# A graph layer on one core: two groups of edges move from GpSimd's gather to hand copies, and the first loads are issued earlier

## The chip, the core and the metric

The kernel runs on one core of a Trainium2 chip. The core has TensorE (PE in the profile; PEld is its weight load), VectorE (DVE), ScalarE (ACT), GpSimd (POOL) and SyncE (SP), each with an instruction stream of its own that runs strictly in order, and 16 DMA engines that move data between HBM and the core's own memory. The metric is device time of one execution in microseconds (us). Three runs of the kernel before took 3376.49, 3378.95 and 3381.35 us; the median, 3378.95 us, is the time before.

## What is computed

One message-passing layer over N = 12,500 nodes and E = 400,000 edges, sorted by target node `dst`. Cut to what matters:

```python
h = relu(layernorm(x))                                  # N x 128
m = relu(concat(h[src], h[dst], edge_attr) @ w1 + b1) @ w2 + b2
agg = segment_sum(m, dst)                               # N x 128
# a GRU cell with input agg and state h, and a residual
gi, gh = agg @ w_ih + b_ih, h @ w_hh + b_hh
r, z = sigmoid(gi_r + gh_r), sigmoid(gi_z + gh_z)
n = tanh(gi_n + r * gh_n)
out = x + (1 - z) * n + z * h
```

`src` is random, so `h[src]` is a gather of 400,000 rows. `dst` is sorted, so the edges of a stretch have their targets in a small window of nodes.

## The kernel before, in words

**First stage (lines 354 to 488).** A loop over chunks `q` of four blocks of 128 nodes normalizes x, keeps hᵀ for all nodes in `hT_all` (128 features on the partitions, one column of 4 bytes for each node), and stores A = h·w1a and B = h·w1b + b1 in HBM. A row of A is what the source of an edge adds to its hidden layer, a row of B what its target adds. `batch_store` (line 253) writes the first three batches of B in this stage; later batches come from the node steps. `at_row` (line 419) loads the source numbers of the groups that are fetched by hand, three rows for each q.

**Edges.** The edges are cut in NP = 391 groups of 1024 (`PAIR` = 8 tiles of 128; group 0 has 5 tiles), and each group is two units u = 2k, 2k+1, so there are NU = 782 units. The main loop (line 1075) goes over u; `stages(u)` (line 1040) holds the work of several units at different depths: the one-hot of target places (`onehot_T`, `onehot`), the products of `pre(u + 3)`, the sums of `add(u + 2)` or `relu(u + 2)`; `seg(u)` then sums over the edges of a node. Everything is in program order on each engine; nothing is reordered at run time. Seven steps `u = -7 .. -1` of `stages` fill the pipe.

For each group three loads are needed. `fetch(q)` (line 567) brings the target places and edge features of two groups to a tile `L`, two DMAs on SP's queue. `window_rows(k)` (line 600) brings the 32-row windows of B to `RW[k % 4]`, two DMAs on SP's queue, from addresses that SP reads to registers, a block of 14 groups at a time. The third is the source part, by one of four ways (`mode`, line 91):

- *GpSimd's gather* (the groups not in `mode`): `gather(k)` (line 151) issues 8 indirect DMAs on POOL, one for each tile of 128 edges, to one of GBUFS = 11 buffers `G`. The first RAW = 9 groups gather rows of x, which are normalized on the spot, since A is not there yet; all others gather rows of A. VectorE adds them in `add` (line 713), behind a wait for their landing.
- *ScalarE by hand* ("act", 28 groups): ACT copies one column of `hT_all` for each of the 1024 edges, at an address in a register (line 979), to `HE_act`; PE then multiplies it by w1a (line 694) and ACT applies the relu (line 725) in place of VectorE's addition.
- *VectorE by hand* ("dve", 27 groups): as ACT, but two columns of bytes in an instruction (line 986), and a copy that puts the bytes in order for each 128 edges (line 991), to `HE_dve`.
- *SP by hand* ("sp", 5 groups): 1024 single-row DMAs from A (line 968) to `G_sp`; VectorE adds as for GpSimd.

A hand job for group k is spread evenly over the units from the end of the engine's job before (`START` for the first: unit 4 for ACT, 14 for DVE) to unit 2k - 4 (`run_jobs`, line 1007: four times in each unit, so many steps that the job is done on time). Before, the groups of ACT end with 374 and 388, those of DVE with 372 and 386, those of SP with 306 and 379. Each hand tile has two buffers, except `G_sp`.

**Nodes.** The targets are cut in 29 blocks (14 groups each but for the last two). When a block's groups are done, `node(b)` (line 790) is run in small steps, one or two units apart: sums over the windows, the gates on PE, sigmoid and tanh on ACT, products on DVE, and the next batch of B. `last_node` (line 857) does the last block.

**Order at the end of the first stage (lines 1032 to 1037):** the first gathers of A, `dst_tile(1)`, three fetches, four `window_rows`; then the seven filling steps.

Of the kernel before, what the change touches and what calls it, by code (L numbers as in the profile page):

```python
# [52 lines left out]
PIECE = 128  # L53
STEP = {"act": 4, "dve": 8, "sp": 4}
ROW = 4 * D
SPREAD = {"dve": 27, "act": 28, "sp": 5}
START = {"dve": 14, "act": 4, "sp": 24}
NR = 12672

H_AT = 16512  # L60

# [2 lines left out]
def tile_gnn(ctx: ExitStack, tc: tile.TileContext, x, src, srcT, dstT, dstP, eaT, eaP, w1, b1, w2T, b2,  # L64
# [23 lines left out]
        return [(t0 + a * GRP + j, j, a) for j in (2 * h, 2 * h + 1) for a in range(2)  # L88
                if t0 + a * GRP + j < t1]

    mode, order = {}, {m: [] for m in SPREAD}
    for m, n in SPREAD.items():
        lo, hi = START[m] // 2 + 2, NP - {"dve": 5, "act": 3, "sp": 12}[m]
        for i in range(n):
            k = lo + int((i + 1) * (hi - lo) / n)
            while k in mode:
                k += 1
            mode[k] = m
            order[m].append(k)


    src_i = {}
# [86 lines left out]
    nc.vector.memset(brow, 0.0)  # L189
    b1b = const.tile([128, D], F32, name="b1b")  # L190
    base_d = at[96:97, :NP - 1]
    by_hand = [k for m in ("sp", "act", "dve") for k in order[m]]
    NJ = len(by_hand)
    place_of = const.tile([NJ, 2], F32, name="place_of")
    for i, (to_sp, to_others) in enumerate(((ROW, 4), (0, H_AT))):
# [107 lines left out]
    def setup(pool):  # L303
# [45 lines left out]
        yield  # L349
        place(0)  # L350

    st_all = const.tile([128, NT, 2], F32, name="st_all")
    nc.vector.memset(st_all[:, NFULL, :], 0.0)
    with tc.tile_pool(name="pp", bufs=3) as pp:
# [85 lines left out]
        for q in range(NC + 3):  # L440
            if q < NC:
                b, i0, c, e, P, n0 = chunk(q)
                if c == 0:
                    stat(b + 2)
                    fin(b + 1)
            if 1 <= q <= NC:
                b, i0, c, e, P, n0 = chunk(q - 1)
                pts[q - 1] = SEGB[q % 2]
                for j in range(c, e):
                    nc.tensor.transpose(pts[q - 1][:, (j - c) * P:(j - c + 1) * P],  # L450
                                        xs[b][:P, j, :], ident[:P, :P])
                if e == bats[b][1]:
                    load(b + 5)
            if q >= 3:
                b, i0, c, e, P, n0 = chunk(q - 3)
                if c == 0:
                    asb[b] = pp.tile([128, 8, D], F32, name="asb", bufs=2)
                nc.scalar.copy(asb[b][:P, c:e, :], pas.pop(q - 3)[:P, :e - c, :])
            if q < NC:
                b, i0, c, e, P, n0 = chunk(q)  # L460
                for j in range(c, e):
                    relu_norm(xs[b][:P, j, :], xs[b][:P, j, :], st_all[:P, i0 + j, :])
                if e == bats[b][1]:
                    sqr(b + 2)
            if 1 <= q <= NC:
                b, i0, c, e, P, n0 = chunk(q - 1)
                copy = nc.scalar.copy if q % 4 == 0 else nc.vector.tensor_copy
                copy(columns(b, c, e), pts.pop(q - 1)[:, :(e - c) * P].rearrange(
                    "f (i p) -> f i p", i=e - c))
            if q >= 4:  # L470
                for _ in range(3):
                    at_row()
            if q >= 6:
                next(setting, None)
            if q in (6, 8, 10):
                batch_product(q // 2 - 3, pp, "bt", 1)
            if q in (7, 9, 11):
                batch_store(q // 2 - 3)
            if q >= 3:
                b, i0, c, e, P, n0 = chunk(q - 3)  # L480
                if e == bats[b][1]:
                    nc.sync.dma_start(nodes(A, i0, e, P), asb[b][:P, :e, :])
            if 2 <= q <= NC + 1:
                b, i0, c, e, P, n0 = chunk(q - 2)
                pas[q - 2] = ps2.tile([128, PAIR, D], F32, name="pre")
                for j in range(c, e):
                    nc.tensor.matmul(pas[q - 2][:P, j - c, :], columns(b, j, j + 1)[:, 0, :],
                                     w1a, start=True, stop=True)
# [72 lines left out]
        nc.vector.tensor_copy(flag, f[:, 6:7])  # L561


    Ls, OH, RT, HE, SEG = ({} for _ in range(5))
    hand = {}

    def fetch(q):
        if q * QP >= NP:
            return
        n = min(QP, NP - q * QP)  # L570
        c = slice(q * QP * 512, (q * QP + n) * 512)
        Ls[q] = p3.tile([128, QP * 512], F32, name="L")
        p = dstP[:, c]
        nc.sync.dma_start(
            Ls[q].bitcast(I32)[:2 * V, :n * 512],
            bass.AP(tensor=p.tensor, offset=p.offset, ap=[list(p.ap[0]), [0, V], [1, n * 512]]))
        nc.sync.dma_start(Ls[q][2 * V:, :n * 512], eaP[:, c])

    def onehot_T(k):
        if k >= NP:  # L580
# [8 lines left out]
                                    accum_out=dlast[:2 * V, n:n + 1])  # L589


    bases = {}

    def block(k):
        return max(b for b in range(NB) if BLOCKS[b][0] <= k)

    def slot(b, i):
        return i // 2 if b < NB - 1 else (BP - BLOCKS[b][1]) // 2 + i // 2

    def window_rows(k):  # L600
        if k >= NP:
            return
        b = block(k)
        k0, n, _ = BLOCKS[b]
        if k == k0:
            _, vals = nc.values_load_multi_w_load_instructions(
                base_i[0:1, b, 0:n], engines=[ET.SP], min_val=0, max_val=4 * D * LAST,
                skip_runtime_bounds_check_because="clamped above")
            for i, v in enumerate(vals):
                bases[k + i] = v  # L610
        v = bases.pop(k)
        for a in range(2):
            nc.sync.dma_start(RW[k % 4].bitcast(U8)[V * a:V * (a + 1), a, :],
                              B_bytes[bass.ds(v + 4 * D * SHIFT * a, 4 * D * V)].rearrange(
                                  "(p f) -> p f", p=V))

    def onehot(k):
        if k >= NP or (k % 2 and k > 1):
# [330 lines left out]
    def one_by_one(m, k):  # L949
        et = {"act": ET.Activation, "dve": ET.DVE, "sp": ET.SP}[m]  # L950
        r = by_hand.index(k)
        if m == "sp":
            goal[k] = tc.alloc_semaphore(f"brought{r}"), 16 * PAIR * 128
            G[k] = pj.tile([128, GRP, 2, D], F32, name="G_sp", bufs=1)
            rows = G[k].bitcast(U8)
        else:
            hand[k] = pj.tile([128, PAIR * 128], F32, name=f"HE_{m}")
            he = hand[k].bitcast(U8)
        for e0 in range(0, PAIR * 128, LOAD[m]):
            low, high = (0, ROW * (N - 1)) if m == "sp" else (H_AT, H_AT + 4 * (N - 1))  # L960
            _, vals = nc.values_load_multi_w_load_instructions(
                at[r:r + 1, e0:e0 + LOAD[m]], engines=[et], min_val=low, max_val=high,
                skip_runtime_bounds_check_because="src holds numbers of nodes")
            if m == "sp":
                for i, v in enumerate(vals):
                    e = e0 + i
                    a, j = divmod(e // 128, GRP)
                    fetched = nc.sync.dma_start(rows[e % 128:e % 128 + 1, j, a, :],
                                                A_bytes[bass.ds(v, ROW)].rearrange("(o f) -> o f", o=1))
                    fetched.then_inc(goal[k][0], 16)  # L970
                    tc.no_tile_sem_insts.add(fetched.ins.name)
                    tc.add_to_no_dep_group(f"rows{k}", fetched.ins)
                    if i % STEP[m] == STEP[m] - 1:
                        yield
                continue
            if m == "act":
                for i, v in enumerate(vals):
                    e = e0 + i
                    nc.scalar.copy(he[:, e * 4:e * 4 + 4], column(v))  # L979
                    if i % STEP[m] == STEP[m] - 1:  # L980
                        yield
                continue
            if e0 % PIECE == 0:
                both = pj.tile([128, PIECE // 2, 4], U16, name="both")
            for i in range(0, LOAD[m], 2):
                nc.vector.scalar_tensor_tensor(both[:, (e0 % PIECE + i) // 2, :], column(vals[i + 1]),  # L986
                                               256.0, column(vals[i]), op0=ALU.mult, op1=ALU.add)
                if i % STEP[m] == STEP[m] - 2:
                    if (e0 + i + 2) % PIECE == 0:
                        p0 = e0 + LOAD[m] - PIECE  # L990
                        nc.vector.tensor_copy(  # L991
                            he[:, p0 * 4:(p0 + PIECE) * 4].rearrange("p (n c b) -> p n c b", c=2, b=4),
                            both.bitcast(U8).rearrange("p n (b c) -> p n c b", c=2))
                    yield
# [12 lines left out]
    def run_jobs(u, phase):  # L1007
        if phase == 0:
            for m, k, span in jobs.get(u, ()):
                live[m] = [one_by_one(m, k), u, span, PAIR * 128 // STEP[m], 0]  # L1010
        for m, job in list(live.items()):
            it, start, span, steps, done = job
            want = -(-steps * ((u - start) * PH + phase + 1) // (span * PH))
# [16 lines left out]
            pass  # L1030

    gathers(0)
    dst_tile(1)
    for q in range(3):
        fetch(q)
    for k in range(4):
        window_rows(k)


    def stages(u):  # L1040
# [248 lines left out]
```

## Time and profile before

| | us |
|---|---|
| median of the runs | 3378.95 |
| the profiled execution, its own time | 3383.87 |
| its span (first to last instruction) | 3382.1 |
| granted TensorE clock, mean over the span | 0.795 of full |
| ACT busy | 3081.1 |
| POOL busy | 2542.8 |
| PE busy (matmuls) | 2400.4 |
| DVE busy | 2213.6 |

The page of the profile has the busy time of each engine, its groups of instructions by line with the mean time of one, and what ended the engine's idle time before them. "issue" there means that the engine waited for no other work that the profile shows, but for its own instruction stream (reading registers, making up a DMA). The timeline has instructions in order of time, neighbours of one kind merged; the number in square brackets is the idle time before, with the instruction that ended it. A table of windows has the busy time of each engine in a stretch of the span.

### The profile page before, as it was taken

The numbers are of one execution on the slowest core, as the hardware profiler recorded it, in microseconds if no ns is written. First come the engines' busy times: TensorE is split into PE (matmuls) and PEld (weight loads), VectorE is DVE, ScalarE is ACT, GpSimd is POOL, SyncE is SP. The second block draws the span as 40 slices with busy tenths as digits, with TensorE's granted clock in tenths as the row PEclk, the third lists the DMA queues.
The fourth block names the chain that finished last, engine by engine and source line by source line (L and its number), as shares of the span: only waits on it lengthen the run. The fifth ranks groups of instructions, "written<-read, shape, count | busy, mean of one in ns | idle before, by whom it ended". The sixth has DMA issues, their size and how long they took to land. (4 is left out here: it accounts for less than half of the span.)

```text
span 3382.1 us, 93395 instructions
## 1 busy us (share of the span) xinstructions
PE 2400.4 (71%) x13113; PEld 1554.8 (46%) x13113; DVE 2213.6 (65%) x16274; ACT 3081.1 (91%) x29057; POOL 2542.8 (75%) x2654
## 2 busy tenths in 40 slices
PE   7567766776677677668776777677667767766767
PEld 6444444444444444445444444444444444444445
DVE  8566666766666666666667766666656666666665
ACT  7599899999999998998999999999889998988975
POOL 7777777777777777777777777777777777777775
PEclk9778777887888777877877878787777787778778
DMA  6433444444444444444444444444444444343332
GB/s 215 104 92 84 95 99 101 99 97 103 96 95 99 97 98 95 99 104 97 96 98 97 98 95 105 97 99 98 95 98 96 100 95 99 94 96 94 92 94 67
DMA packets 196737, 335.77 MB, mean 99 GB/s; under 512 B 69445, under 2 KB 118148, under 8 KB 196112
## 3 DMA queue, kind: packets, MB, share of 16 engines
q0 software_dynamic: 84640, 173.51, 23.0%
q1 hardware_dynamic: 111327, 156.18, 17.8%
q14 instruction: 517, 4.23, 0.4%
q8 instruction: 109, 1.79, 0.2%
q10 hardware_dynamic: 144, 0.07, 0.0%
HBM read 309.25 MB, written 20.24 MB: 97 GB/s over the span
## 5 line engine op out<-in xcount | busy, mean ns | idle before, releaser
L163 POOL DMA_INDIRECT G<-A,src_i x2576 | 2475.8, 961 | 790.4 <-issue 761.2
L979 ACT COPY HE_act<-hT_all 128x4 uint8 x28672 | 2889.0, 189 | 52.9 <-issue 29.1
L986 DVE SCALAR_TENSOR_TENSOR both<-hT_all 128x4 uint16 x13824 | 1174.3, 154 | 930.3 <-issue 925.6
L683 PE MATMUL pre<-RW,L 128*128 128x256 f32 x3128 | 1136.1, 489 | 461.3 <-DMA RW<-B 237.7
L683 PEld LDWEIGHTS pre<-RW,L 128*128 128x128 f32 x3128 | 662.8, 237 | 736.8 <-issue 420.2
L739 PE MATMUL seg<-RB,OH 128*32 128x129 f32 x6250 | 592.7, 319 | 244.2 <-DVE RB L713 211.9
L739 PEld LDWEIGHTS seg<-RB,OH 128*32 128x32 f32 x6250 | 328.0, 123 | 590.7 <-DVE RB L713 310.1
L713 DVE CUSTOM_DVE_ANT_0 RB<-pre,G 128x1024 f32<-128x1024 f32 x323 | 391.1, 1211 | 70.9 <-DMA G<-A,src_i 56.5
L586 DVE TENSOR_SCALAR L<-L,node_of 64x512 f32<-64x512 int32 x382 | 185.9, 487 | 62.2 <-DMA L<-in_dstP 59.9
L725 ACT ACTIVATE RB<-pre 128x1024 f32<-128x1024 f32 x64 | 65.0, 1016 | 91.0 <-PE pre L694 91.0
L633 DVE TENSOR_TENSOR OH<-dloc,seg 128x512 f32<-128x512 f16 (+1 forms) x198 | 132.3, 669 | 0.0
L765 PE MATMUL nd<-spot,sums 128*128 128x40 f32 x782 | 119.6, 326 | 3.6 <-DVE sums L748 3.6
L765 PEld LDWEIGHTS nd<-spot,sums 128*128 128x128 f32 x782 | 115.5, 237 | 12.7 <-issue 8.8
L991 DVE COPY HE_dve<-both 128x512 uint8<-128x512 uint8 x216 | 97.6, 452 | 7.4
L244 PE MATMUL nd<-w1b,hT_all 128*128 128x128 f32 x224 | 49.4, 368 | 73.1 <-DVE xb L850 73.1
L734 PE MATMUL seg<-zrow 1*128 1x129 bf16 x196 | 45.5, 232 | 78.1 <-DVE OH L633 78.0
L694 PEld LDWEIGHTS pre<-w1a,HE_dve 128*128 128x128 f32 x432 | 89.1, 255 | 12.4
L694 PEld LDWEIGHTS pre<-w1a,HE_act 128*128 128x128 f32 x448 | 85.9, 238 | 11.0
L694 PE MATMUL pre<-w1a,HE_dve 128*128 128x128 f32 x432 | 85.4, 333 | 0.0
L694 PE MATMUL pre<-w1a,HE_act 128*128 128x128 f32 x448 | 83.7, 319 | 0.0
L163 POOL DMA_INDIRECT G<-in_x,src_i x69 | 65.6, 950 | 21.9 <-issue 20.7
L244 PEld LDWEIGHTS nd<-w1b,hT_all 128*128 128x128 f32 x224 | 35.2, 231 | 85.5 <-DVE xb L850 80.0
(177 smaller groups left out, 1346.2 us busy)
## 6 DMA issues: line engine op xcount, KB each, us to landing
G_sp<-A SPq DMA_DIRECT2D x5120, 0.5 KB
L<-in_dstP SPq DMA_DIRECT2D x195, 256.0 KB
L<-in_eaP SPq DMA_DIRECT2D x195, 256.0 KB
G<-A,src_i POOLq DMA_INDIRECT x2576, 2.5
RW<-B SPq DMA_DIRECT2D x782, 16.0 KB
xb<-in_x SPq DMA_DIRECT2D x26, 256.0 KB
out<-xb SPq DMA_DIRECT2D x26, 256.0 KB
xs<-in_x SPq DMA_DIRECT2D x11, 512.0 KB
```

The lines of the kernel that those rows point to most:

```text
L163: fetched = nc.gpsimd.indirect_dma_start(out=G[k][:, j, a, :], out_offset=None, in_=table, in_offset=bass.IndirectOffsetOnAxis(ap=src_i[c] ...
L244: nc.tensor.matmul(pm[:m, i:i + D], hT_all[:, n0 + i:n0 + i + m], w1b, start=True, stop=True)
L586: nc.vector.tensor_scalar(o, i, node_of[:, k:k + 1], None, op0=ALU.is_equal)
L633: nc.vector.tensor_tensor(p, dloc[:, e0:e1, None].to_broadcast(shape), row[:, None, :].to_broadcast(shape), op=ALU.is_equal)
L683: nc.tensor.matmul(p[:, 2 * i:2 * i + 2, :], Ls[k // QP][:, c0:c0 + 128], RW[k % 4], start=True, stop=not raw)
L694: nc.tensor.matmul(p[:, 2 * i + a, :], cols, w1a, start=False, stop=n + 1 == len(l) or l[n + 1][1] != j)
L713: made = nc.vector._custom_dve(TENSOR_ADD_SAT, out=o, in0=p, in1=G[k].rearrange("p j a f -> p (j a) f")[:, c, :], s0=float("inf"), s1=0.0)
L739: nc.tensor.matmul(p[r0:r0 + V, :D + 1], OH[k][:, a * GRP + j, :], RB[k % 2][:, 2 * j + a, :D + 1], start=False, stop=all(b != a for _, _, ...
L765: nc.tensor.matmul(p[:, bass.ds(offs[i], V + SHIFT)], sums[:, slot(b, i), :D], spot[:, i % 2, :], start=False, stop=i == len(offs) - 1)
L979: nc.scalar.copy(he[:, e * 4:e * 4 + 4], column(v))
L986: nc.vector.scalar_tensor_tensor(both[:, (e0 % PIECE + i) // 2, :], column(vals[i + 1]), 256.0, column(vals[i]), op0=ALU.mult, op1=ALU.add)
L991: nc.vector.tensor_copy(he[:, p0 * 4:(p0 + PIECE) * 4].rearrange("p (n c b) -> p n c b", c=2, b=4), both.bitcast(U8).rearrange("p n (b c) ...
```

## The change

Two things are changed.

1. *The first loads.* `fetch(0)` is issued at q = 4 of the first stage, on ScalarE's queue, to a buffer of `HE_dve` (the tile pool of `L` does not exist yet at that point). The four first `window_rows` are issued at q = 16 of that stage, on SP's queue as before. After the first stage only `fetch(1)` and `fetch(2)` are left, now ahead of `dst_tile(1)`.
2. *The groups by hand.* ACT gets 29 groups in place of 28, DVE 27 as before, and both share group 385 (`SHARED` = NP - 6): ACT copies its edges 0 to 511 and DVE its edges 512 to 1023, to one tile `HE_dve`. GpSimd's gather thus has two groups fewer. The jobs are spread anew so that both engines end with group 385: ACT's jobs are 13 groups apart in most cases (13 or 14 before, 13.7 on the average), DVE's 13 or 14 (14 before). ACT's last jobs are 365, 379 and half of 385; DVE's 364, 378 and half of 385; SP's five are 85, 156, 228, 299, 371. Groups 386 to 390 all go to GpSimd.

```diff
-SPREAD = {"dve": 27, "act": 28, "sp": 5}
+SPREAD = {"dve": 27, "act": 29, "sp": 5}
 START = {"dve": 14, "act": 4, "sp": 24}
+SHARED, CUT = NP - 6, 512
...
-    mode, order = {}, {m: [] for m in SPREAD}
+    def share(m, k):
+        return (0, PAIR * 128) if k != SHARED else (0, CUT) if m == "act" else (CUT, PAIR * 128)
+
+    mode, order = {SHARED: "both"}, {m: [] for m in SPREAD}
     for m, n in SPREAD.items():
-        lo, hi = START[m] // 2 + 2, NP - {"dve": 5, "act": 3, "sp": 12}[m]
+        lo, hi = START[m] // 2 + 2, NP - 20
+        part = 0
+        if m != "sp":
+            hi, part = SHARED, (share(m, SHARED)[1] - share(m, SHARED)[0]) / (PAIR * 128)
         for i in range(n):
-            k = lo + int((i + 1) * (hi - lo) / n)
+            k = lo + int((i + 1) * (hi - lo) / (n + part))
             while k in mode:
                 k += 1
             mode[k] = m
             order[m].append(k)
+        order[m] += [SHARED] if part else []
...
+        if q == 0:
+            Ls[q] = pj.tile([128, QP * 512], F32, name="HE_dve")
+        else:
+            Ls[q] = p3.tile([128, QP * 512], F32, name="L")
         p = dstP[:, c]
+        queue = nc.scalar if q == 0 else nc.sync
...
+            if q == 16:
+                for k in range(4):
+                    window_rows(k)
+            if q == 4:
+                fetch(0)
...
-            hand[k] = pj.tile([128, PAIR * 128], F32, name=f"HE_{m}")
+            if k not in hand:
+                hand[k] = pj.tile([128, PAIR * 128], F32, name="HE_dve" if k == SHARED else f"HE_{m}")
...
-        for e0 in range(0, PAIR * 128, LOAD[m]):
+        for e0 in range(*share(m, k), LOAD[m]):
...
     gathers(0)
+    for q in (1, 2):
+        fetch(q)
     dst_tile(1)
-    for q in range(3):
-        fetch(q)
-    for k in range(4):
-        window_rows(k)
```

The definitions of `fetch`, `window_rows`, `block` and `bases` move ahead of the first stage, otherwise unchanged.

More of the change, by code (lines that the diff above doesn't have):

```diff
@@ L191, in tile_gnn @@
     base_d = at[96:97, :NP - 1]
-    by_hand = [k for m in ("sp", "act", "dve") for k in order[m]]
+    by_hand = order["sp"] + order["act"] + [k for k in order["dve"] if k != SHARED]
     NJ = len(by_hand)
@@ L350, in setup, with fetch, block, window_rows @@
         place(0)
+    Ls = {}
+    def fetch(q):
+        if q * QP >= NP:
+            return
+        n = min(QP, NP - q * QP)
+        c = slice(q * QP * 512, (q * QP + n) * 512)
+        if q == 0:
+            Ls[q] = pj.tile([128, QP * 512], F32, name="HE_dve")
+        else:
+            Ls[q] = p3.tile([128, QP * 512], F32, name="L")
+        p = dstP[:, c]
+        queue = nc.scalar if q == 0 else nc.sync
+        queue.dma_start(
+            Ls[q].bitcast(I32)[:2 * V, :n * 512],
+            bass.AP(tensor=p.tensor, offset=p.offset, ap=[list(p.ap[0]), [0, V], [1, n * 512]]))
+        queue.dma_start(Ls[q][2 * V:, :n * 512], eaP[:, c])
+    bases = {}
+    def block(k):
+        return max(b for b in range(NB) if BLOCKS[b][0] <= k)
+    def window_rows(k):
+        if k >= NP:
+            return
+        b = block(k)
+        k0, n, _ = BLOCKS[b]
+        if k == k0:
+            _, vals = nc.values_load_multi_w_load_instructions(
+                base_i[0:1, b, 0:n], engines=[ET.SP], min_val=0, max_val=4 * D * LAST,
+                skip_runtime_bounds_check_because="clamped above")
+            for i, v in enumerate(vals):
+                bases[k + i] = v
+        v = bases.pop(k)
+        for a in range(2):
+            nc.sync.dma_start(RW[k % 4].bitcast(U8)[V * a:V * (a + 1), a, :],
+                              B_bytes[bass.ds(v + 4 * D * SHIFT * a, 4 * D * V)].rearrange(
+                                  "(p f) -> p f", p=V))
     st_all = const.tile([128, NT, 2], F32, name="st_all")
@@ L561, in check_windows @@
         nc.vector.tensor_copy(flag, f[:, 6:7])
-    Ls, OH, RT, HE, SEG = ({} for _ in range(5))
+    OH, RT, HE, SEG = ({} for _ in range(4))
     hand = {}
[L567 to L577, printed above, removed]
     def onehot_T(k):
@@ L589, in onehot_T @@
                                     accum_out=dlast[:2 * V, n:n + 1])
-    bases = {}
-    def block(k):
-        return max(b for b in range(NB) if BLOCKS[b][0] <= k)
     def slot(b, i):
         return i // 2 if b < NB - 1 else (BP - BLOCKS[b][1]) // 2 + i // 2
[L600 to L615, printed above, removed]
     def onehot(k):
@@ L1009, in run_jobs @@
             for m, k, span in jobs.get(u, ()):
-                live[m] = [one_by_one(m, k), u, span, PAIR * 128 // STEP[m], 0]
+                e0, e1 = share(m, k)
+                live[m] = [one_by_one(m, k), u, span, (e1 - e0) // STEP[m], 0]
         for m, job in list(live.items()):
```

## The prediction

> **What bounds the kernel now.** I read the page first, for the busy times, then GpSimd's gather line by itself, because its mean period says more than its busy share.
>
> ```profile
> span 3382.1 us, 93395 instructions
> PE 2400.4 (71%) x13113; PEld 1554.8 (46%) x13113; DVE 2213.6 (65%) x16274; ACT 3081.1 (91%) x29057; POOL 2542.8 (75%) x2654
> L979 ACT COPY HE_act<-hT_all 128x4 uint8 x28672 | 2889.0, 189 | 52.9 <-issue 29.1
> L986 DVE SCALAR_TENSOR_TENSOR both<-hT_all 128x4 uint16 x13824 | 1174.3, 154 | 930.3 <-issue 925.6
> L991 DVE COPY HE_dve<-both 128x512 uint8<-128x512 uint8 x216 | 97.6, 452 | 7.4
> L725 ACT ACTIVATE RB<-pre 128x1024 f32<-128x1024 f32 x64 | 65.0, 1016 | 91.0 <-PE pre L694 91.0
> ```
> ```profile
> L163 POOL DMA_INDIRECT G<-A,src_i x2576: 940/944/1601, 92.8 to 3355.0; - x199
> L163 POOL DMA_INDIRECT G<-in_x,src_i  x69: 940/945/1097, 3.4 to 88.7; - x69
> ...
>   issue: 781.9, 2564
>   DVE both L986: 7.6, 25
>   DVE RB L713: 5.2, 17
>   PE misc L666: 3.3, 4
>   DMA L<-in_dstP: 3.2, 1
> ```
>
> POOL looks 75% busy, yet it starts 2645 gathers from 3.4 to 3355.0 us without a pause: (3355.0 - 3.4) / 2644 = 1.268 us each, of which 0.94 is counted busy and 0.30 is "issue". The only real waits are 3.2 us (the stores of A) and 3.3 us (a buffer); the short rows behind DVE are the same 0.3 us of issue that ended beside something else. So POOL sets the end: its last gather is followed by 3382.1 - 3355.9 = 26.2 us of tail. A group of eight gathers costs 10.1 us.
>
> Whether anything can take over those groups is a question to ACT, which at 91% is the fullest engine. Its waits between its first and last copy, with the ends of that stretch:
>
> ```profile
> ACT RB L725 <- PE pre L694: 86.9, 25, 12.4
> ACT gt L824 <- PE nd L818: 63.3, 19, 9.0
> ACT HE_act L979 <- issue: 29.1, 79, 1.2
> ACT gt L834 <- DVE both L986: 4.2, 1, 4.2
> ACT gt L836 <- PE misc L818: 2.0, 1, 2.0
> ```
> ```profile
> 142.61 1.23 ACT L979 COPY HE_act<-hT_all 128x4 uint8 x12
> ...
> 3345.26 2.37 ACT L979 COPY HE_act<-hT_all 128x4 uint8 x24
> 3351.76 1.02 ACT L725 ACTIVATE RB<-pre 128x1024 f32<-128x1024 f32 x1 [4.12 <-PE pre L694]
> ```
>
> From 142.6 to 3347.6 are 3205.0 us, and in them ACT waits for others only 86.9 + 63.3 + 4.2 + 2.0 = 156.4 us; the other 3048.6 are work and issue. That number decides the case. The waits are spread over the whole run, not a reserve at one place. VectorE is as full, as the middle of the run shows (busy time by window, then its waits there):
>
> ```profile
> core 0: us, PE busy (x) PEld busy (x) DVE busy (x) ACT busy (x) POOL busy (x), PEclk, DMA share, GB/s
> ...
> 1000.00:2250.00 1250.00, 893.57 (x4910) 563.96 (x4905) 834.29 (x6263) 1187.28 (x11484) 948.92 (x987) 0.80 0.42 98
> ```
> ```profile
> DVE both L986 <- issue: 366.6, 312, 3.1
> DVE L L586 <- DMA L<-in_dstP: 24.9, 12, 5.2
> DVE TOT L776 <- PE nd L765: 7.9, 3, 2.7
> DVE RB L713 <- PE pre L683: 7.9, 8, 3.1
> ```
>
> Busy plus the reading of registers ("issue" at line 986) is 834.3 + 366.6 = 1200.9 of 1250 us, 96.1%; the waits for others are about 43 us. ACT there has 1187.3 of 1250, 95.0%. No wait for a gather stands in this list: consumption runs behind POOL there, at its own pace, and only later catches up with it.
>
> **The first loads.** The timeline behind the first stage:
>
> ```profile
> 81.62 8.06 SPq L482 DMA_DIRECT2D A<-asb  x4
> ...
> 90.21 0.66 SPq L574 DMA_DIRECT2D L<-in_dstP  x1
> ...
> 100.32 0.48 DVE L586 TENSOR_SCALAR L<-L,node_of 64x512 f32<-64x512 int32 x1 [9.76 <-DMA L<-in_dstP]
> ...
> 118.39 1.19 PE L683 MATMUL pre<-RW,L 128*128 128x256 f32 x2 [11.73 <-DMA RW<-B]
> ...
> 122.61 0.69 DVE L668 COPY gt<-misc 128x512 f32<-128x512 f32 x1 [11.77 <-PE misc L666]
> ...
> 124.86 0.94 POOL L163 DMA_INDIRECT G<-A,src_i  x1 [2.34 <-PE misc L666]
> ```
>
> DVE waits 9.76 us for the first L; then PE waits 11.73 us for the first RW, and DVE 11.77 for PE. With L and RW loaded during the first stage both go: 9.76 + 11.77 = 21.5 us earlier for PE, DVE and ACT. What could be late next is L of groups 2 and 3, wanted at about 100 us; it now leaves first behind the stage, as the first L did at 90.2, which was there 10.1 us later, so I add nothing for it. On ACT the move adds two issues at q = 4, which I cost by the same two on SP (0.58 and 0.51 us, quoted below); ACT is not what bounds that stage, and without that cover they cost 1.1 us. On SP eight RW issues (0.41 each, 3.3 us) and one read of registers move ahead of A's last stores; POOL's first gather of A hangs on those, but SP has room there: its last four stores are spread over 8.06 us, with no other issue between. Bounds for the move: 0 us gained (the loads land no earlier) to 21.5. I take 21.5, since both stalls name the loads that are moved, and 25 and 13 steps q of the first stage (29 of them in some 89 us, 3 us each) now lie between issue and end of the stage. POOL gains its buffer wait of 2.3 us.
>
> Here the Trainium skill (DMA: Bandwidth & Descriptors, "Issuing engines are not separate DMA queues") speaks against the queue half of the edit: DMAs of all issuing engines run on the same 16 DMA engines, and another issuer saves only issue time. By that rule alone the ScalarE queue is worth the 1.1 us of two issues, and the rest of the 21.5 must come from the earlier place; the sum is the same.
>
> **The two groups moved.** POOL loses 16 gathers, 16 x 1.268 = 20.3 us. With the buffer wait its last gather ends at 3355.9 - 22.6 = 3333.3, and by POOL alone the span would be 3359.5.
>
> ACT gains 1.5 jobs: 1536 copies at (2889.0 + 29.1) / 28672 = 101.8 ns, 156.3 us, and two relus more (lines 725, 1.0 us each). Work from first to last copy: 3048.6 + 156.3 + 2.0 = 3206.9 us. That is all of the 156.4 us in which it waited: from now on ACT alone fills the loop. First copy at 142.6 - 21.5 = 121.1, last copy without any wait at 3328.0.
>
> DVE gains half a job, (1174.3 + 925.6 + 97.6) / 27 / 2 = 40.7 us, less two additions of 1.2 us. Against ACT's 158 us it stays below: its 3.9% of waits in the middle are some 120 us over the run, so DVE is not the bound, but has little left. PE gains 32 products of hand groups, which lie in its idle 29%.
>
> SP's five jobs are spread over some 133 units in place of 136:
>
> ```profile
> 547.37 0.58 SPq L574 DMA_DIRECT2D L<-in_dstP  x1
> 548.01 0.51 SPq L577 DMA_DIRECT2D L<-in_eaP  x1
> 548.63 5.20 SPq L968 DMA_DIRECT2D G_sp<-A  x16
> 553.93 0.81 SPq L613 DMA_DIRECT2D RW<-B  x2
> 554.85 7.30 SPq L968 DMA_DIRECT2D G_sp<-A  x16
> ```
>
> 32 rows take 12.5 us, a job 400 us, 6.0 us for each of 66.5 groups; with 0.8 for RW and half of 1.1 for L about 7.4 us a group, under the 8.4 that ACT needs (worked out below). Not the bound either.
>
> **The tail.** ACT's last copy stood at unit 772 and now stands at unit 766, three groups earlier; what follows it is longer.
>
> ```profile
> 3356.16 1.22 DVE L713 CUSTOM_DVE_ANT_0 RB<-pre,G 128x1024 f32<-128x1024 f32 x1 [1.50 <-PE pre L683]
> ...
> 3361.10 1.29 DVE L713 CUSTOM_DVE_ANT_0 RB<-pre,G 128x512 f32<-128x512 f32 x2 [3.15 <-PE pre L683]
> ```
>
> From the relu of 388 (3351.76) to the addition of 390 (3361.10), PE and DVE without hand jobs took 9.3 us for two groups, 4.7 a group. Three groups more are 14 us: 3382.1 - 3347.6 + 14 = 48.5 us behind the last copy.
>
> **The sum.** 121.1 + 3206.9 + 48.5 = 3376.5 us of span if ACT never waits. It will: a relu or a sigmoid stands behind PE, and all copies stand behind it. Bounds: zero, and the 41 us that ACT waits in 1250 in the middle, 3.3%, or 106 us over 3207. I take 18 us, near the lower end: ACT needs 3206.9 / 29.5 = 108.7 us for the 13 groups of a job. In the middle window ACT's 11484 instructions are some 11.1 jobs of 13.7 groups, 152 groups, so DVE needs 1200.9 / 152 = 7.9 us a group, with the new half job 8.0, 104 us for 13. The lead of 4.7 us a job just holds DVE's own stalls, 43 / 11.1 = 3.9, so ACT rarely finds PE late. 3394.5 us of span is 12.4 above the span of before. The profiled execution was 1.8 us longer than its span and 4.9 above the median; carried over, 3391 us, 0.4% slower.
>
> **Rivals.**
> *ACT keeps up and POOL still ends last (faster).* It decides if ACT's last copy comes by 3311 (3359.5 - 48.5), 17 us before my no-wait sum: a shorter tail, or copies that cost less than 101.8 ns in closer rows. For it: PE never waits for line 979 in the trace. Against it: 156.4 us of waits cannot be shed below zero. 3356 us, chance 0.15.
> *No wait at all on ACT*: 3373 us, next to no change, chance 0.20.
> *The first loads gain nothing* (L or RW late for another reason): 21.5 more than forecast, 3412 us, chance 0.08.
> *Three full engines hold each other up as in the middle*: 106 us of waits, 3479 us, chance 0.08. Against it: part of ACT's waits there only show that it was ahead.
> *The halves of group 385 wait for each other*, as both write one tile: DVE's 40.7 us follow ACT's half, 3432 us, chance 0.04. They write other columns.
> *ACT was the bound all along*: 3382.1 - 21.5 + 158.3 + 14 = 3533 of span, 3530 us, chance 0.03; its 156 us of waits and POOL's unbroken 1.268 us speak against it. The Trainium skill (Perfetto Trace Analysis, "Identifying the Most-Contended Engine") names the engine of highest occupancy as the bottleneck; here that would be ACT, and the trace does not agree, since POOL's 0.30 us between gathers are not free time.
>
> **How the numbers follow.** The forecast (waits of 6 to 45 us, 3379 to 3418) has 0.42. A measurement of this kernel can tell some 0.2%, 6.8 us, from no change. Faster by more: POOL's case and a third of the no-wait case, 0.22. Within 0.2%: the rest of the no-wait case and the lowest part of the forecast's, 0.20. Slower: 0.58. For 8 in 10 the range goes from 3356, which leaves out half of POOL's case, to 3433, which leaves out the two dearest; as it holds both signs, the forecast's own range of 3379 to 3418 stands beside it.
>
> **What would show it.** The first L and RW stalls gone and ACT's first copy near 121 us. 2629 gathers, still 1.268 us apart, the last near 3333. ACT's waits in the loop down from 156 us to some 20, its last copy near 3346, 12 us or more after POOL's end, and PE waiting for line 979 before hand groups. The sum falls if ACT's waits stay above 60, if the last copy comes before 3320, or if POOL waits for buffers.

## The result, and the profile after

The changed kernel took 3422.19 us (median of 4 runs, 3418.65 to 3428.17) beside 3379.61 us for the kernel before on the same chip: a ratio of 1.0128, 95% interval 1.0115 to 1.0141. It is slower, by 42.6 us where 12 were forecast. The profiled execution took 3418.65 us, the lowest of the four.

The page and GpSimd's and ScalarE's lines, first and last start behind the colon:

```profile
span 3416.9 us, 95323 instructions
PE 2444.2 (72%) x13145; PEld 1565.8 (46%) x13145; DVE 2232.5 (65%) x16532; ACT 3242.0 (95%) x30595; POOL 2525.9 (74%) x2638
L999 ACT COPY HE_act<-hT_all 128x4 uint8 x29696 | 3001.0, 189 | 59.4 <-issue 35.1
```
```profile
L171 POOL DMA_INDIRECT G<-A,src_i x2560: 940/945/1563, 99.0 to 3337.4; - x197
```
```profile
L999 ACT COPY HE_act<-hT_all x29696: 177/189/199, 128.6 to 3312.2; 128x4 uint8 x200
L999 ACT COPY HE_dve<-hT_all x512: 180/189/195, 3312.4 to 3366.6; 128x4 uint8 x171
...
  PEld pre L713: 6.5, 3
  PE pre L713: 5.9, 3
```

GpSimd's last gather ends at 3338.3, 78.5 us ahead of the end (26 before): it no longer sets it. ScalarE copies from 128.6 to 3366.8, and now PE waits for its copies ("who waited for it", the two rows of line 713), which it never did before. What ScalarE itself still waited for in that stretch, then its tail:

```profile
ACT HE_act L999 <- issue: 35.1, 126, 1.1
ACT gt L843 <- PE nd L837: 12.5, 5, 4.8
ACT RB L744 <- PE pre L713: 7.7, 4, 5.1
ACT gt L853 <- DVE gt L850: 2.5, 2, 1.9
```
```profile
3339.28 27.51 ACT L999 COPY HE_dve<-hT_all 128x4 uint8 x272 [0.27 <-issue]
3367.33 0.44 ACT L843 ACTIVATE gt<-nd 128x320 f32<-128x320 f32 x1 [0.54 <-PE nd L837]
3372.87 1.02 ACT L744 ACTIVATE RB<-pre 128x1024 f32<-128x1024 f32 x1 [5.11 <-PE pre L713]
...
3405.71 0.44 ACT L926 ACTIVATE gt<-pre 128x320 f32<-128x320 f32 x1 [26.78 <-PE pre L907]
```

12.5 + 7.7 + 2.5 = 22.7 us, where there were 156.4. The other 3238.2 - 22.7 = 3215.5 us are work, 166.9 more than before (158 were forecast): 133.7 of them went into ScalarE's waits, of which little is left, and 33.2 made the stretch of its copies longer. Behind its last copy come 3416.9 - 3366.8 = 50.1 us, 15.6 more than before, and its first copy comes 14.0 us earlier: 33.2 + 15.6 - 14.0 = 34.8 us, the difference of the two spans. The last row is a 27 us wait for the groups that all had to follow group 385.

The stage before the loop shows something that was not in the forecast. First a store of A on SP's queue, before and after; then who waited in the stage behind it:

```profile
26.56 0.37 SPq L482 DMA_DIRECT2D A<-asb  x1
```
```profile
25.50 0.86 SPq L471 DMA_DIRECT2D at<-in_src  x3
35.82 0.37 SPq L535 DMA_DIRECT2D A<-asb  x1
```
```profile
22.78 1.15 ACTq L373 DMA_DIRECT2D HE_dve<-in_dstP  x1
...
23.97 0.52 ACTq L376 DMA_DIRECT2D HE_dve<-in_eaP  x1
...
38.80 0.59 ACT L506 COPY asb<-pre 128x512 f32<-128x512 f32 x1 [5.20 <-DMA A<-asb]
```
```profile
SPq L535 <- DMA HE_dve<-in_dstP: 9.4, 1, 9.4
```
```profile
POOL G L171 <- DMA A<-asb: 9.4, 1, 9.4
```
```profile
97.92 0.47 DVE L627 TENSOR_SCALAR HE_dve<-HE_dve,node_of 64x512 f32<-64x512 int32 x1
```

SP stands for 9.4 us and waits for the early load of the places, which ScalarE issued at 22.78 and which landed at 35.76. The store does not use what that load brings. It has the same completion semaphore (number 133 in the trace), and goes out at 35.82, right after the landing. Everything behind it in SP's queue, the stores of A among them, shifts; ScalarE waits 5.2 us for its buffer, and the first gather of A starts at 99.0 (92.8 before). The old stalls are gone: VectorE's first use of L, the last row, is at 97.92 with no wait in brackets, and PE's first product of RW starts at 104.06 without one, where it started at 118.39.

### The profile page after: what moved, and what is told of

Read it like the earlier page. It is cut to its first block, busy times and chain, and to the rows that moved or that the text cites. A ratio compares the mean times of both kernels' runs of the same rounds, so it can differ in the third digit from the quotient of the medians.

```text
span 3416.9 us, 95323 instructions
## 1 busy us (share of the span) xinstructions
PE 2444.2 (72%) x13145; PEld 1565.8 (46%) x13145; DVE 2232.5 (65%) x16532; ACT 3242.0 (95%) x30595; POOL 2525.9 (74%) x2638
## 5 line engine op out<-in xcount | busy, mean ns | idle before, releaser
L999 ACT COPY HE_act<-hT_all 128x4 uint8 x29696 | 3001.0, 189 | 59.4 <-issue 35.1
L1006 DVE SCALAR_TENSOR_TENSOR both<-hT_all 128x4 uint16 x14080 | 1190.9, 153 | 975.5 <-issue 969.2
L702 PEld LDWEIGHTS pre<-RW,L 128*128 128x128 f32 x3112 | 672.0, 241 | 567.1 <-issue 350.4
L758 PE MATMUL seg<-RB,OH 128*32 128x129 f32 x6250 | 612.6, 328 | 335.9 <-DVE RB L732 248.3
L784 PE MATMUL nd<-spot,sums 128*128 128x40 f32 x782 | 110.0, 310 | 1.2 <-DVE sums L767 1.1
L784 PEld LDWEIGHTS nd<-spot,sums 128*128 128x128 f32 x782 | 105.6, 219 | 9.9 <-issue 8.2
L833 PE MATMUL nd<-DEG,brow 34*128 34x512 f32 (+2 forms) x112 | 69.9, 707 | 24.7 <-ACT gt L843 24.2
L713 PEld LDWEIGHTS pre<-w1a,HE_dve 128*128 128x128 f32 x448 | 81.2, 226 | 9.4
```

Source lines behind the costliest of these rows:

```text
L702: nc.tensor.matmul(p[:, 2 * i:2 * i + 2, :], Ls[k // QP][:, c0:c0 + 128], RW[k % 4], start=True, stop=not raw)
L713: nc.tensor.matmul(p[:, 2 * i + a, :], cols, w1a, start=False, stop=n + 1 == len(l) or l[n + 1][1] != j)
L758: nc.tensor.matmul(p[r0:r0 + V, :D + 1], OH[k][:, a * GRP + j, :], RB[k % 2][:, 2 * j + a, :D + 1], start=False, stop=all(b != a for _, _, ...
L784: nc.tensor.matmul(p[:, bass.ds(offs[i], V + SHIFT)], sums[:, slot(b, i), :D], spot[:, i % 2, :], start=False, stop=i == len(offs) - 1)
L833: nc.tensor.matmul(pg, brow[:, c], DEG[:, :w], start=True, stop=False)
```

## The experiments

All times are medians beside runs of the kernel before on the same chip. The first four runs and the last four went to chips on which that kernel took 3378.5 and 3378.4 us; the four between went to another, told of at the end.

**The first loads alone.** The groups as before (28 on ScalarE, 27 on VectorE, none shared, old spacing):

```diff
-SPREAD = {"dve": 27, "act": 29, "sp": 5}
+SPREAD = {"dve": 27, "act": 28, "sp": 5}
-SHARED, CUT = NP - 6, 512
+SHARED, CUT = -1, 512
```

> The first loads as changed, the groups by hand as before (28, 27 and 5, none shared). Theory (in the changed kernel ACT is the bound; the first loads hold up the first stage by some 7.5 us because a store on SP waits 9.4 us for the early L): with POOL as the bound again only its own start counts, 9.4 us of wait instead of 3.2 ahead of the first gather of A, 2.3 us of buffer wait gone: span 3386, ratio 1.001, POOL's last gather at 3360. Rival (the earlier first loads move the whole kernel ahead by 14 us or more): span 3368 or less, ratio 0.996.

3380.88 us, ratio 1.0009 [1.0000, 1.0018]. ScalarE's first copy comes at 129.6 instead of 142.6, and the time is not shorter for it:

```profile
L169 POOL DMA_INDIRECT G<-A,src_i x2576: 940/944/1524, 99.3 to 3349.0; - x199
```
```profile
ACT RB L742 <- PE pre L711: 100.9, 26, 11.5
ACT gt L841 <- PE nd L835: 39.9, 14, 8.2
```

GpSimd starts its gathers of A at 99.3 instead of 92.8 and runs without a pause, and its last gather ends 24 us ahead of the end, as before (26). ScalarE still waits 145.4 us for others (the two rows and 4.6 for VectorE). But its work between first and last copy is 3064.9 us where it was 3048.6; these 16 us are told of further down, and they used up the 13 us gained. So this run alone does not show that ScalarE was not the bound; GpSimd's unbroken gathers and the next run do.

**The groups alone.** Loads and first rows as before, groups as in the change:

```diff
-            if q == 16:
-                for k in range(4):
-                    window_rows(k)
-            if q == 4:
-                fetch(0)
...
-        queue = nc.scalar if q == 0 else nc.sync
+        queue = nc.sync
```

> The groups by hand as changed, the first loads as before. Theory (ACT is the bound): first copy back at 142.6, 3238 us to the last copy, 50 us of tail: span 3431, ratio 1.0145, some 14 us above the changed kernel. Rival (the first loads are what made the changed kernel slow, by the held-up first stage): span 3382 or less. Rival (POOL is still the bound): POOL's last gather at 3336, span 3362.

3432.74 us, ratio 1.0169 [1.0153, 1.0184]. So the loss is the groups', and the early loads gave back 10.5 us of it (3432.74 - 3422.19), half of what was put down to them. The loss is 54 us on this chip, though ScalarE got 158 us of copies and a tail of three more groups: it was not the bound of the kernel before, GpSimd was.

**The early places in two loads.** The load that takes the long landing reads two rows of 4 KB, each repeated to 32 partitions. Here each row has its load:

```diff
+        if q == 0:
+            for a in range(2):
+                pa = dstP[a:a + 1, c]
+                queue.dma_start(
+                    Ls[q].bitcast(I32)[V * a:V * (a + 1), :n * 512],
+                    bass.AP(tensor=pa.tensor, offset=pa.offset, ap=[[0, V], [1, n * 512]]))
```

> The changed kernel with the places of the early L brought by two DMAs, one for each half of the group, each from one row repeated 32 times, in place of one DMA from two rows. Theory (the one DMA takes 13 us to land because its two rows use few DMA engines, and SP's next store of A has to wait for its landing): landing within 6 us, the store's wait under 2 us, first stage as long as before, ACT's first copy at 121 to 123, span 3410, ratio 1.009. Rival (the 13 us are the load of all DMA engines in that stage, or ScalarE's queue): the store waits 7 us or more again, span 3417.

3415.68 us, ratio 1.0117 [1.0102, 1.0132], 6.5 us under the changed kernel's median. The intervals of the two overlap, so the time alone does not show a gain; the trace does. SP's queue:

```profile
25.73 2.04 SPq L478 DMA_DIRECT2D at<-in_src  x3
27.88 0.37 SPq L542 DMA_DIRECT2D A<-asb  x1
```

The store is back at 27.88, the first gather at 93.3, ScalarE's first copy at 123.5 instead of 128.6. By the trace's record of their semaphores, the two loads landed 4.8 and 5.0 us after their issue (22.73 to 27.54, 23.10 to 28.05), where the one load took 13.0.

**The early places on SP's queue.**

```diff
-        queue = nc.scalar if q == 0 else nc.sync
+        queue = nc.sync
```

> The changed kernel, but its early fetch of the first places and features issued from SP's queue in front of all else, not from ScalarE's. If it is the reuse of a completion semaphore by SP's later load, not ScalarE's queue as such, that stops SP at the first store of A, the store stands where the landing of that load still is 13 us after its issue, and since the issue is earlier by some 10 us relative to the store or later by its own place, either the stop goes (store at 26 to 28 us, first copy on ScalarE near 121 to 124) or it stays 3 to 9 us. Rival (the issue from ScalarE itself, 1.7 us, and the order of ScalarE's work make the stage longer): the first copy comes before 124 only because ScalarE issues nothing, and the store of A stands as long as before.

3403.72 us, one run. The place of the load is the same, q = 4, and not ahead of all else as the expectation has it. SP now issues it at 22.43 and stands all the same, a little later in its order: now a load of `at` shares a semaphore with it.

```profile
22.43 0.60 SPq L373 DMA_DIRECT2D HE_dve<-in_dstP  x1
23.08 0.53 SPq L376 DMA_DIRECT2D HE_dve<-in_eaP  x1
...
27.73 0.38 SPq L535 DMA_DIRECT2D A<-asb  x1
28.16 7.81 SPq L471 DMA_DIRECT2D at<-in_src  x3
```
```profile
SPq L471 <- DMA HE_dve<-in_dstP: 6.5, 1, 6.5
```

The second of the three goes out at 34.96, just after the landing at 34.94. The first copy is at 128.5, as in the changed kernel (128.6): the stop comes from the slow landing and the reused semaphore, whichever queue issues the load. And ScalarE's 1.7 us of issuing cost the stage nothing.

Yet the time is 18.5 us under the changed kernel's median and 15 under its lowest run. It is the stretch of ScalarE's copies that got shorter. The same row in four kernels, first two without a load on ScalarE's queue (this one and the groups alone), then two with (the first loads alone, and the split load):

```profile
L999 ACT COPY HE_act<-hT_all 128x4 uint8 x29696 | 2992.4, 189 | 49.8 <-issue 23.4
```
```profile
L991 ACT COPY HE_act<-hT_all 128x4 uint8 x29696 | 2991.7, 189 | 50.2 <-issue 24.3
```
```profile
L997 ACT COPY HE_act<-hT_all 128x4 uint8 x28672 | 2898.5, 189 | 60.5 <-issue 35.1
```
```profile
L1006 ACT COPY HE_act<-hT_all 128x4 uint8 x29696 | 3001.3, 189 | 59.4 <-issue 33.3
```

Busy and idle together: 3042.2 and 3041.9 us for 29696 copies without, 3060.4 (changed kernel) and 3060.7 with; for 28672 copies 2941.9 in the kernel before and 2959.0 with. A single copy keeps its 189 ns, and 18 us over 29696 / 16 = 1856 blocks of 16 copies are 10 ns for each read of 16 registers. The trace has them there: within a block a copy starts 95 ns after the one before in all kernels, but from the last copy of a block to the first of the next it is 195 ns in the changed kernel and 182 to 183 ns in those without the load (medians). The read itself, 1.05 us beside the copies, is no longer. Of the ten kernels of the first and last runs, the seven with an early load on ScalarE's queue have the longer step, 195 to 196 ns, and the three without (the kernel before among them) do not. Why loads at 23 us should lengthen this step for the next 3.3 ms was not found.

**The shared group three groups later.**

```diff
-SHARED, CUT = NP - 6, 512
+SHARED, CUT = NP - 3, 512
```

> The changed kernel with group 388 shared in place of 385. Theory (behind ACT's last copy PE and DVE need 4.7 us for each group that is left): tail of 36 us in place of 50, the stretch of ACT's copies the same 3238 us: span 3403, ratio 1.0075. Rival (the end is set by what PE or DVE have to do, not by ACT's last copy): last copy later by as much as the tail is shorter, span 3417.

3395.16 us, ratio 1.0051 [1.0035, 1.0066], 27 us under the changed kernel; the spans of the profiled executions differ by 32.0 us, where 14 were expected.

```profile
L999 ACT COPY HE_dve<-hT_all x512: 179/189/195, 3300.4 to 3354.4; 128x4 uint8 x171
```
```profile
ACT gt L843 <- PE nd L837: 10.2, 3, 6.1
ACT RB L744 <- PE pre L713: 1.9, 2, 1.4
ACT gt L853 <- DVE gt L850: 1.5, 1, 1.5
```

The last copy ends at 3354.6 and 30.3 us follow instead of 50.1: 19.8 of the 32.0 us are the tail, 6.6 for each of the three groups. ScalarE's jobs lie a little farther apart, and its waits fall to 13.6 us, another 9.1. It stays the bound.

**One job less on ScalarE, then with the two edits above, then one more on VectorE.** The first has 28 and a half groups on ScalarE; the second adds the split load and the later shared group; the third moves one more group from GpSimd to VectorE:

```diff
-SPREAD = {"dve": 27, "act": 29, "sp": 5}
+SPREAD = {"dve": 27, "act": 28, "sp": 5}
```
```diff
-SPREAD = {"dve": 27, "act": 28, "sp": 5}
+SPREAD = {"dve": 28, "act": 28, "sp": 5}
```

> The changed kernel with ScalarE's whole groups back to 28 (28.5 with its half of group 385, as against 29.5), VectorE 27.5, POOL 56. On a chip like that of the first four runs: if ScalarE's copies behind a later first copy set the end of the changed kernel, one job of about 109 us less on ScalarE makes POOL's gathers the last to end again: 2645 - 8 = 2637 gathers of 1.266 us from 99.3, last one near 3339, ScalarE waiting 50 to 60 us, the shared group's half still lying 50 us before the end; span 3370 to 3385, time 3372 to 3388 us, ratio 0.998 to 1.002. Rival (three engines that hold each other up, ScalarE's count does not matter): time stays at 3410 or more, ratio above 1.009. On a slower chip, where ScalarE's issuing bounds all kernels, the time goes by ScalarE's jobs, 28.5 against 28: ratio near 1.014.

> As the run with 28 and a half on ScalarE, with the early places fetched in two loads (first gather of A near 93.3 instead of 99.1) and the shared group three groups later in the order. On a chip like that of the first four runs: POOL's last gather near 93.3 + 2637 x 1.266 = 3332, tail 28 to 30: span 3360 to 3366, time 3362 to 3369 us, ratio 0.995 to 0.997: faster than the kernel before. Rival (the gathers are not what ends last, or the first stage's gain is lost in buffer waits): no change, 3378 or more.

> As the run before it, with one more whole group moved from POOL to VectorE (28.5 on VectorE, 28.5 on ScalarE, 55 on POOL). On a chip like that of the first four runs: POOL's last gather near 93.3 + 2629 x 1.266 = 3322; ScalarE 28.5 jobs of 109 us from 123.5 end near 3250 with waits of 60 more: 3310 to 3330; if VectorE has the room (96% taken in the middle before, one job more of its copies is about 81 us of its time), the end follows POOL: span 3350 to 3358, time 3352 to 3361 us, ratio 0.992 to 0.995. Rival (VectorE becomes the bound and POOL and PE wait for its adds): 3375 or more, with POOL waiting over 40 us for VectorE's adds.

3401.03 us, 1.0068 [1.0054, 1.0082]; 3381.94 us, 1.0011 [1.0002, 1.0020]; 3445.28 us, 1.0203 [1.0189, 1.0217]. All three expectations were too low. The first time lies between its theory and its rival (3410 or more); the second and the third are those of their rivals. With one job less ScalarE waits again (rows of the first, over the whole span), and GpSimd ends at 3346.8, yet 46 us ahead of the end:

```profile
ACT gt L843 <- PE nd L837: 67.2, 15, 8.9
ACT RB L744 <- PE pre L713: 34.2, 13, 9.0
```
```profile
L171 POOL DMA_INDIRECT G<-A,src_i x2568: 940/945/1524, 99.4 to 3345.9; - x198
```

So neither of the two is the bound there. The third run shows one that lies right behind. VectorE from 1000 to 2250 us, its 1250 us window and its waits:

```profile
1000.00:2250.00 1250.00, 868.84 (x4718) 547.06 (x4717) 827.06 (x6345) 1164.90 (x11222) 942.08 (x983) 0.80 0.41 96
```
```profile
DVE both L1013 <- issue: 397.3, 316, 2.4
DVE RB L739 <- PE pre L709: 7.7, 3, 4.7
DVE TOT L802 <- PE nd L791: 3.5, 1, 3.5
DVE both L1013 <- DMA B<-xb: 3.0, 1, 3.0
```

827.1 + 397.3 = 1224.4 of 1250 us: VectorE is the bound now, and one group too many on it costs 63 us. GpSimd's waits for its additions, which the rival put at over 40 us, are 13.6. Worked out from the traces, the pace (time between the first segment products of groups 20 and 380, by 360) and the share of those 1250 us in which an engine waits for no other:

```
                          us a group   ScalarE  VectorE  SP's queue
before                      8.325       96.7%    96.5%    94.6%
changed kernel              8.446       99.7%    96.6%    93.2%
shared group later          8.371       99.4%    96.7%    93.6%
28.5 on ScalarE             8.402       97.2%    97.6%    94.4%
28.5, both edits            8.397       96.0%    96.5%    94.6%
28.5 on each                8.543       95.3%    98.5%    92.8%
```

In the fourth and fifth rows nobody is quite full, and still the pace is behind that of before: in the fifth VectorE waits 38.2 us in the window for L, which SP brings:

```profile
DVE L L634 <- DMA L<-in_dstP: 38.2, 17, 8.6
```

Which of VectorE and SP's queue holds that version was not told apart, and its profiled execution was the slowest of eleven, 9 us above the median. It is level with the kernel before; no version that was run is faster than that.

**On another chip.** There the kernel before took 5701.85 us (17 runs). The three kernels just told of and the load on SP's queue ran there first:

> The changed kernel with 28 whole jobs on ScalarE in place of 29, and one group more for GpSimd; all else as changed. Theory (ACT is the bound of the changed kernel): ACT's copies need 104 us less, so GpSimd's gather is the bound again: 2568 gathers of 1.266 us from 99.0, the last at 3349, span 3375, ratio 0.998, ACT's waits between its copies above 60 us. Rival (VectorE, SP and PE hold each other up, and ACT only shows it): span 3405 or more, ACT's waits below 40 us or its last copy within 20 us of before.

> Early places in two DMAs, group 388 shared in place of 385, 28 whole jobs on ScalarE and 27 on VectorE: one group fewer for GpSimd than before the change. Theory (GpSimd's gather is the bound, and the first stage is as long as before): first gather of A at 93.3, 2568 gathers of 1.266 us, the last at 3343, span 3369, ratio 0.997. Rival (the full engines behind it set the end): span 3380 or more, last addition over 25 us behind the last gather.

> As the run with one group moved, but with 28 whole jobs on VectorE too: two groups fewer for GpSimd, as in the change, the second on VectorE in place of ScalarE. Theory (ACT alone was the bound, VectorE has 130 us of slack for 81 us more): GpSimd's gather is the bound, last gather at 3333, span 3359, ratio 0.994. Rival (VectorE, 96% full, becomes the bound as ACT did): span 3380 or more, its waits for loads and products near zero, ACT waiting for PE.

> The changed kernel with the early L issued at the same place on SP's queue in place of ScalarE's. Theory (a later DMA on the same completion semaphore has to wait for the slow load, whichever queue issued it): SP stands still for some 9 us in the first stage again, ACT's first copy at 127 to 130. Rival (ScalarE's queue makes it slow): the wait is gone, first copy at 121 to 123.

In that order: 1.0142 [1.0120, 1.0164], 1.0146 [1.0124, 1.0168], 1.0005 [0.9993, 1.0017], and 5841.13 us in one run. The expectations were made for a chip like the first and are not met. The page of the first of them:

```profile
L999 ACT COPY HE_act<-hT_all 128x4 uint8 x28672 | 3172.2, 190 | 2170.3 <-issue 2143.5
L171 POOL DMA_INDIRECT G<-A,src_i x2568 | 2453.4, 955 | 3116.4 <-DVE RB L732 2202.8
```

A copy takes its 190 ns there too, but ScalarE idles 2143.5 us by "issue" (38.1 us for the same kernel on the chip of the last four runs), and GpSimd waits 2200 us for buffers. Between its first and last copy ScalarE waits less than 2 us for others in all four runs: with this idle time it is the bound of these kernels there, and they say nothing of a choice between GpSimd and ScalarE. The idle time stands before copies at every place of a block of 16 (a copy starts 170 to 190 ns after the one before on the average, 95 in the median), so it is not the reading of registers, which takes 1.05 us on both chips. The third kernel has the same copies on ScalarE as the second, and of the 77 us between their times 69 are this idle time (2154.8 and 2086.0); why one more VectorE group in place of a gather's does that stays open. The load on SP's queue tells nothing of the stop there: it was issued at 64.8 and landed at 72.5, long before SP came to a DMA with its semaphore.

## Why the prediction was right, and where its sizes were off

The direction and the mechanism held: GpSimd was the bound, the 158 us of copies went into ScalarE's 156 us of waits, ScalarE became the bound, and the tail grew behind group 385. The time, 3422, is 31 us over the forecast of 3391, inside the range of 3356 to 3433 and just outside the likeliest case's own 3379 to 3418. Of the signs that it named, ScalarE's waits of some 20 us, PE's waits for its copies and its end well behind GpSimd's came; its last copy came at 3366.8 and not near 3346.

The sum by its terms, in the profiled execution:

- *First copy*, 121.1 forecast, 128.6 measured: +7.5. Both stalls went, as said; what failed was "I take 21.5, since both stalls name the loads that are moved". It asked what the loads no longer stop, and not what the early load itself stops: 9.4 us on SP's queue. With the load split the first copy comes at 123.5. The sentence on the queues had SP's room for more issues right, and missed that a landing can hold a queue too. GpSimd's expected 2.3 us of gain became a loss of 6.2 at its first gather, so its last one ended at 3338.3 and not near 3333.
- *ScalarE's work without waits*, 3206.9 forecast, 3238.2 - 22.7 = 3215.5 measured: +8.6. Without the load on ScalarE's queue it is 128.5 to 3350.3 less 25.3 of waits, 3196.5. The forecast counted the move to ScalarE's queue at 1.1 us of issue; it costs ScalarE 18 to 19 in the stretch of its copies, and without it the term would have come out 10 us under the forecast: part of the agreement is luck. No row of the trace of before could show that.
- *Residual waits*, 18 forecast, 22.7 measured: +4.7. The argument that VectorE just keeps ahead of 13 groups a job fits: with 96.6% of its time taken at 8.446 us a group VectorE needs 8.16 us, where 8.0 were forecast.
- *Tail*, 48.5 forecast, 50.1 measured: +1.6. This is luck, as the later shared group shows: with group 388 the tail was 30.3 and not the 34.5 taken from the kernel before, and three groups more were 19.8 us and not 14. The two errors nearly cancel.

Together +22.4 on 3394.5 of span, the 3416.9 measured. The rest of the 31 us is that the profiled run was the lowest of the changed kernel's, where the one before was taken 4.9 us above its median.

The rivals: *ACT keeps up* fell with the 78 us between the last gather and the end. *No wait at all* fell by 22.7 us and by the larger work. *The first loads gain nothing* fell in the form it had, since 10.5 us of their gain are there. *Three full engines hold each other up* fell for the changed kernel, whose ScalarE waits 3.5 us of the middle 1250; with 28.5 groups on ScalarE something like it is left. *The halves wait for each other* fell: between its copies for group 385 ScalarE shows only the 0.27 us of issue quoted above, and VectorE's half was done at 3363.9, 3 us ahead of ScalarE's. *ACT was the bound all along* fell with the time, 3422 and not 3530, and with the groups alone, which cost 54 us.

One bound was too generous: "about 7.4 us a group, under the 8.4 that ACT needs" puts SP's queue at 88%; in the middle of the run it waits for no other in 93.2% of the time (94.6% before). The expectations for 28.5 groups went by GpSimd and ScalarE, and left out the same thing: SP's queue at 94% and VectorE at 96%, which only the third named, as a rival.

## What to carry to other kernels

Where one engine sets the end and the others wait 3 to 5%, look at what each waits for before work is handed on: 156 us of waits were all that ScalarE had to give, 167 us of work were given to it, and the 20 us taken from GpSimd bought nothing. Count for a moved load also its landing, and who shares its completion semaphore. And put a shared last job where little follows it: three groups later were worth 27 us here.

## What was not expected of the hardware

The early load of two rows repeated over 64 partitions took 13 us from issue to landing (22.78 to 35.76, and 12.5 us on the other queue), and stopped a queue that had no use for it. The page "DMA: Bandwidth & Descriptors" of the Trainium skill ("Why a DMA increments its semaphore by 16 and not by 1", on the number of engines) says that a transfer is spread over the largest number of engines, up to 16, that divides the slowest dimension of both its sides; worked out from that rule, two rows over 64 partitions would leave two. The trace agrees: behind a step at the end of its issue (24.02) the load's semaphore has only two more before the store is issued, at 33.98 and 35.76, while each of the two loads of one row has sixteen, and these removed the stop.

Loads issued from ScalarE's queue at the start go with 16 to 22 us more in the stretch of its copies, some 12 ns at each read of 16 registers, in all kernels of the first and last runs that have them.

The kernel before took 3378 us on one chip and 5702 on another. In the one with 28.5 groups on ScalarE, which has a trace from both, a copy takes 189 and 190 ns, the granted clock is 0.80 and 0.67, and ScalarE idles 38 and 2144 us by "issue" before its copies.
